# Turning normed attention inputs by 32x32 blocks and a trip through memory instead of on the matrix engine

## The chip, the cores and the metric

The kernel runs on one core of a Trainium2 chip. The metric is the device time of one execution in microseconds (us). Before the change it is 941.15 us, the median of three runs (940.75 to 942.05).

A core has a matrix engine (TensorE, PE in the profile, PEld for its weight loads), three engines for elementwise work (VectorE or DVE, ScalarE or ACT, GpSimd or POOL), a queue engine (SyncE or SP) that issues transfers here, and sixteen DMA engines that carry them. Each engine works through its own instructions in order; semaphores tie them together.

## The reference

For each of 16 batches (256 tokens, 256 features, 16 heads of 16) three attentions follow one another, and a feed-forward layer ends it. All is float32.

```python
x0  = rmsnorm(x + softmax(rms(x)Wq (rms(y)Wk)' * scale) rms(y)Wv Wo)   # layer 0: cross attention
h   = layernorm(x0);  q, k, v = h@sa_w...;  rope(q), rope(k)
x1  = x0 + softmax(causal(q k' * scale)) v @ sa_wo                     # layer 1: causal, on itself
h   = layernorm(x1);  q = h@ca_wq;  k, v = y@ca_w...;  rope(q), rope(k)
x2  = x1 + softmax(q k' * scale) v @ ca_wo                             # layer 2: cross attention
out = x2 + gelu(layernorm(x2)@fc1) @ fc2
```

## The kernel before, in words

There are 48 attentions (3 layers x 16 batches), worked off in a list `ORDER` of layer numbers written by hand, in one loop `for i in range(N_ATT)`. After it come eight feed-forward groups of two batches. The emission order is the order of each engine: the schedule is manual.

In loop `i` TensorE does attention `i` in blocks: four score blocks for layers 0 and 2, three for the causal layer 1 (L472 scores, then L511 values of the block before). A non-causal loop takes 15.2 to 16.2 us, a causal one 13.3. Between the blocks it does the dense work of neighbouring attentions:

- block 0: the last values of `i-1`; on VectorE, the statistics (L236, L237; on POOL L218, L219) of `i+2`, the copy of the values of `i-1` out of PSUM (L528), the normalization of `i+2` (L243), and the division of `i-2` (L562). Then the queries of `i+1` (`by_feature`, L274), with their rotation on VectorE (L386 to L408).
- block 1: the keys of `i+1` (L274, rotation to L431); the inverse of the softmax sums of `i-1` (L548).
- next to last block: the values' weights of `i+1` (`by_token`, L287, L452).
- last block: the output projection of `i-2` (L287, added by L568 or L571), then the **turn** of `i+2`.

In a loop whose attention `i-3` was of layer 0 (`finishing`) that one's last scaling (L576) comes in block 0, and the normalization of `i+2` in block 1.

The turn matters here. The dense matmuls want the input with features on partitions (`hT`), but layernorm (`ln_apply`) leaves tokens on partitions (`xn`). For layers 1 and 2, `turned` makes four 128x128 transposes on TensorE into a PSUM bank (L254) and a ScalarE copy into `hT` (L259), a tile `[P, KC, S]` in two buffers. Layer 0 needs none: its input comes already turned from the host. So 32 attentions have a turn. The queries of layers 1 and 2 and the keys and values of layer 1 read `hT`; keys and values of layer 2 read `yT`.

The head outputs and the softmax sums go through memory, by SP: stores of the values (L529), reads of the sums (L536) and of the head outputs (L541), a store of the inverted sums (L550) and its spread reads (L556). Inputs of later batches and weights are issued on SP in `load_next` (L903), right after the reads of L541 and again in block 1.

The buffers: `A`, where values accumulate, has one PSUM bank, freed by L528. Score tiles have two. Dense results have three banks. Tile `a`, in which rotations start, has two buffers.

Of the kernel before, what the change touches and what calls it, by code (L numbers as in the profile page):

```python
# [32 lines left out]
PT_LIVE = 6  # L33

# [8 lines left out]
SWAP = [(i // HD) * HD + (i + HD // 2) % HD for i in range(32)]  # L43

@with_exitstack
def xattn_kernel(
# [202 lines left out]
    def turned(src, name, pool, tag, bufs):  # L249

        ps = dense_ps()
        for c in range(NC):
            for k in range(KC):
                nc.tensor.transpose(  # L254
                    ps[:, k * S + c * P : k * S + (c + 1) * P],
                    src[:, c, k * P : (k + 1) * P], ident,
                )
        t = pool.tile([P, KC, S], F32, tag=tag, name=name, bufs=bufs)
        nc.scalar.copy(t.rearrange("p k s -> p (k s)"), ps)  # L259
        return t  # L260

# [6 lines left out]
    def by_feature(src, w, at, ts=range(KC)):  # L268

        ps = dense_ps()  # L270
        for t in ts:
            for k in range(KC):
                for j in range(0, P, 32):
                    nc.tensor.matmul(  # L274
                        ps[j : j + 32, t * S : (t + 1) * S],
                        lhsT=w[:, k, at + t * P + j : at + t * P + j + 32], rhs=src[:, k, :],
                        start=(k == 0), stop=(k == KC - 1), skip_group_check=True,
                    )
        return ps.rearrange("p (t s) -> p t s", s=S)

    def by_token(src, w, at):

        ps = dense_ps()
        for c in range(NC):
            for k in range(KC):
                for j in range(0, P, 32):
                    nc.tensor.matmul(  # L287
                        ps[j : j + 32, c * D : (c + 1) * D],
                        lhsT=src[:, k, c * P + j : c * P + j + 32], rhs=w[:, k, at : at + D],
                        start=(k == 0), stop=(k == KC - 1), skip_group_check=True,  # L290
                    )
        return ps.rearrange("p (c d) -> p c d", d=D)


    class Att:
        def __init__(self, i):
            self.i = i
            self.layer = ORDER[i]
            self.b = ORDER[:i].count(self.layer)
            self.causal = self.layer == 1  # L300
            self.w = (w0_sb, sa_sb, ca_sb)[self.layer]
            self.w_o = (w0o_sb, sao_sb, cao_sb)[self.layer]
            self.x = rows_of(self.b)
            self.va = vas[i % 2]


            if self.causal:
                self.blocks = [[(0, 0)], [(0, 1), (1, 1)], [(1, 0)]]
                self.parts = [[(0, 0)], [(0, 1)], [(1, 1), (1, 0)]]
            else:  # L310
                self.blocks = [[(t, kc)] for t in range(KC) for kc in range(NC)]
                self.parts = self.blocks
            self.pts = {}
# [56 lines left out]
        def turn(self):  # L370
            if self.layer == 0:
                self.hT = xTs.pop(self.b)
            else:
                self.hT = turned(self.xn, "hT", work, "hT", 2)
            self.kvT = self.hT if self.layer == 1 else yTs[self.b]
# [207 lines left out]
    def att(i):  # L583
        if 0 <= i < N_ATT:
            return atts.setdefault(i, Att(i))
        return None
# [43 lines left out]
    class Mlp:  # L630
# [15 lines left out]
        def turn(self, copy=nc.scalar.copy):  # L646
            self.hT = self.pool.tile([P, KC, 2, S], F32, tag="qm", name="hT3")
            for i, xn in enumerate(self.xns):
                ps = dense_ps()
                for c in range(NC):  # L650
                    for k in range(KC):
                        nc.tensor.transpose(  # L652
                            ps[:, k * S + c * P : k * S + (c + 1) * P],
                            xn[:, c, k * P : (k + 1) * P], ident,
                        )
                copy(self.hT[:, :, i, :], ps.rearrange("p (k s) -> p k s", s=S))

        def mix(self, tag="av"):
# [5 lines left out]
            else:  # L664
                pairs = [self.pool.tile([P, 2, S], F32, tag=tag, name="ts") for _ in range(2)]
# [196 lines left out]
    with tc.manual_schedule():  # L862
# [42 lines left out]

        for i in range(N_ATT):
            a, last = att(i), att(i - 1)
            ahead = att(i + 3)
            if i > 1 and ahead is not None and ahead.layer == 0:
# [5 lines left out]
            follows = (  # L915
                finishing and i + 2 < N_ATT
                and att(i + 2).layer == 1 and att(i + 2).b == att(i - 3).b
            )
            for n in range(len(a.blocks)):
                if n == 0 and a.causal and not finishing:  # L920
                    do(i + 2, "stats")
# [6 lines left out]
                if n == 0:  # L928
# [4 lines left out]
                    if not follows and not late and (finishing or not a.causal):  # L933
                        do(i + 2, "stats")
                    do(i - 1, "end")
                    load_next(i)
                    if late:
                        do(i + 2, "stats")
                    do(i - 3, "finish")
                    if follows:  # L940
                        do(i + 2, "stats")
                    if not finishing:
                        do(i + 2, "norm")
# [9 lines left out]
                elif n == 1:  # L953
# [11 lines left out]
                    if finishing:  # L965
                        do(i + 2, "norm")
# [5 lines left out]
                if n == final - 1:  # L972
                    do(i + 1, "v")
                    if i == N_ATT - 2:
                        mlps[1].stats()
                    if i == N_ATT - 1:
                        mlps[0].up(2)
                        mlps[0].mix("hT")
                if n == final:
# [4 lines left out]
                    do(i + 2, "turn")  # L984
# [16 lines left out]
                if i == 2 and n == 2:  # L1001
                    att_cols = fold_back(att_hop)
                    row_v = ctile([P, D], "row_v")
# [505 lines left out]
```

## Time and profile before

| | |
|---|---|
| median of three runs | 941.15 us |
| the profiled execution | 940.73 us |
| its span (first to last instruction) | 939.0 us |
| TensorE busy | 929.7 us |
| VectorE / ScalarE / POOL busy | 662.7 / 547.1 / 311.4 us |
| turns on TensorE (L254) | 128 transposes, 272 to 330 ns each, overlapping |
| copies of turned inputs (L259) | 32, 586 ns each |
| normalization (L243) | 96 of 593 ns |
| statistics (L236, L237) | 96 of 405 ns, 96 of 182 ns |
| matmuls that read `hT` (L274) | 1,536 of 379 ns each, overlapping |
| transfers | 83.2 MB in 98,989 packets |

The busy time of an engine is the union of its instructions. Matmuls overlap: four that write different groups of 32 partitions run at once, so what one costs is read from the distance between starts, not from its duration. The profile follows a chain back from the last instruction: at each step to what released it, or to the instruction before it on its engine. A loop's length is read from the timeline of TensorE, as the distance between the first L472 of one attention and of the next.

### The profile page before, as it was taken

The page shows a single profiled execution, that of the slowest core. Times are in us where ns is not written, and L with a number is a line of the kernel's source. Part 1 is how long each engine was busy: PE and PEld are TensorE (multiplying, and loading weights), DVE is VectorE, ACT ScalarE, POOL GpSimd, SP SyncE. Part 2 cuts the span into 40 slices and gives each one's busy share as a digit, 9 for nine tenths or more (in the row PEclk, how much of TensorE's full clock was granted, in tenths as well). Part 3 has the DMA queues.
Part 4 walks back from the last instruction along what each step waited for, and adds up shares of the span by engine and source line. Part 5 has one row for each costly group of instructions (what it writes and reads, how often), then busy time and mean ns, then how long its engine had stood idle before and what let it go on. Part 6 is the DMA issues. An engine that isn't in the chain of part 4 may idle for free.

```text
span 939.0 us, 29252 instructions
## 1 busy us (share of the span) xinstructions
PE 929.7 (99%) x12358; PEld 548.6 (58%) x12358; DVE 662.7 (71%) x1440; ACT 547.1 (58%) x772; POOL 311.4 (33%) x503
## 2 busy tenths in 40 slices
PE   8999999999999999999999999999999999999997
PEld 3444555445454455455454545455444799999997
DVE  4458776867777787868866768888787576667663
ACT  3666655766666665656656666666666634444440
POOL 4213454125444364253542324445133021222200
PEclk9999999999999999999999999999999999999999
DMA  9434353333333233321443322222212100000001
GB/s 292 155 102 129 120 161 114 118 110 95 110 99 95 82 104 100 106 91 58 136 127 97 110 83 63 79 72 82 82 60 82 38 23 23 13 12 24 24 24 48
DMA packets 98989, 83.20 MB, mean 89 GB/s; under 512 B 21658, under 2 KB 98594, under 8 KB 98850
## 3 DMA queue, kind: packets, MB, share of 16 engines
q1 hardware_dynamic: 98162, 80.70, 27.4%
q8 instruction: 99, 1.62, 0.7%
q10 hardware_dynamic: 688, 0.54, 0.2%
q14 instruction: 40, 0.33, 0.1%
HBM read 51.05 MB, written 30.17 MB: 86 GB/s over the span
## 4 chain that ended last, share of the span: by engine, by line
PE 98%; DMA 1%; DVE 0%; SPq 0%; POOL 0%; issue 0%; ACT 0%; DVEq 0%
PE S L472 20%; PE A L511 19%; PE d L287 17%; PE d L274 17%; PE upX L676 6%; PE A L774 5%; PE downZ L774 3%; PE upZ L676 3%; PE d L254 2%; PE d L774 2%; PE d L676 1%; PE d L652 1%; PE downX L774 1%; DMA y<-in_y 1%; PE d L172 0%; SPq L107 0%
## 5 line engine op out<-in xcount | busy, mean ns | idle before, releaser
L483 ACT ACTIVATE pt<-S 128x1024 f32<-128x1024 f32 x224 | 217.3, 1022 | 120.4 <-PE S L472 120.2
L472 PE MATMUL S<-qm,kT 32*128 32x512 f32 (+1 forms) x1536 | 202.4, 600 | 0.7 <-DVE qm L422 0.4
L511 PE MATMUL A<-pt,va 128*32 128x256 f32 (+1 forms) x3072 | 188.7, 367 | 0.0
L511 PEld LDWEIGHTS A<-pt,va 128*32 128x32 f32 x3072 | 80.0, 109 | 153.4 <-issue 107.1
L483 ACT ACTIVATE pt<-S,sy 128x1024 f32<-128x1024 f32 x128 | 135.8, 1111 | 47.1 <-PE S L472 46.2
L490 POOL TENSOR_SCALAR_AFFINE_SELECT pt<-pt 128x512 f32<-128x512 f32 x128 | 90.3, 721 | 60.1 <-ACT pt L483 59.6
L472 PEld LDWEIGHTS S<-qm,kT 32*128 32x128 f32 x1536 | 62.3, 183 | 66.6 <-issue 40.8
L218 POOL TENSOR_SCALAR r_ln<-bmv 128x2 f32<-128x2 f32 x48 | 13.9, 290 | 217.0 <-DVE bmv L237 215.8
L263 POOL TENSOR_TENSOR cur<-cur,bias 128x512 f32<-128x512 f32 x48 | 66.1, 1382 | 56.5 <-DVE xn L243 56.5
L382 ACT ACTIVATE a<-d,qk_bias 128x256 f32<-128x256 f32 x128 | 53.7, 471 | 51.3 <-PE d L274 39.5
L274 PE MATMUL d<-hT,sa 128*32 128x256 f32 x1024 | 61.1, 379 | 0.0
L571 DVE TENSOR_TENSOR cur<-d,cur 128x512 f32<-128x512 f32 x32 | 22.0, 687 | 50.7 <-PE d L287 50.7
L528 DVE COPY av<-A 128x512 f32<-128x512 f32 x47 | 32.3, 687 | 30.4 <-PE A L511 29.9
L243 DVE TENSOR_SCALAR xn<-cur,bmv,r_ln 128x256 f32<-128x256 f32 x96 | 52.2, 593 | 1.4 <-POOL r_ln L219 0.8
L390 DVE TENSOR_TENSOR u<-u,turn 128x512 f32<-128x512 f32 x64 | 49.7, 777 | 0.0
L390 DVE TENSOR_TENSOR a<-a,turn 128x512 f32<-128x512 f32 x64 | 47.3, 739 | 2.2
L714 ACT ACTIVATE g<-g,fb 128x256 f32<-128x256 f32 x96 | 41.0, 500 | 11.1 <-DVE g L703 11.1
L386 DVE STREAM_SHUFFLE u<-a 128x512 f32<-128x512 f32 x64 | 47.5, 742 | 0.0
L274 PEld LDWEIGHTS d<-hT,sa 128*32 128x32 f32 x1024 | 33.3, 110 | 22.0
L218 POOL TENSOR_SCALAR r_o<-ms_o 128x2 f32<-128x2 f32 x16 | 3.9, 243 | 125.6 <-DVE sq L226 116.0
L562 DVE TENSOR_TENSOR oT<-oT,inv 128x512 f32<-128x512 f32 x48 | 39.6, 824 | 5.8 <-DMA inv<-inv_hop 5.8
L769 DVE TENSOR_TENSOR g<-g,g 128x512 f32<-128x512 f32 x64 | 40.9, 682 | 0.0
(149 smaller groups left out, 1566.4 us busy)
## 6 DMA issues: line engine op xcount, KB each, us to landing
hop<-av SPq DMA_DIRECT2D x96, 256.0 KB
oT<-hop SPq DMA_DIRECT2D x96, 128.0 KB
inv<-inv_hop SPq DMA_DIRECT2D x96, 128.0 KB
xT<-in_xt SPq DMA_DIRECT2D x16, 256.0 KB
cur<-in_x SPq DMA_DIRECT2D x16, 256.0 KB
yT<-in_yt SPq DMA_DIRECT2D x16, 256.0 KB
y<-in_y SPq DMA_DIRECT2D x16, 256.0 KB
out<-res SPq DMA_DIRECT2D x15, 256.0 KB
```

The lines of the kernel that those rows point to most:

```text
L243: nc.vector.tensor_scalar(xn[:, c, :], src[:, c, :], mv[:, c, 0:1], r[:, c : c + 1], ALU.subtract, ALU.mult,)
L263: nc.gpsimd.tensor_tensor(t, t, bias_sb[:, row : row + D].unsqueeze(1).to_broadcast([P, NC, D]), ALU.add)
L274: nc.tensor.matmul(ps[j : j + 32, t * S : (t + 1) * S], lhsT=w[:, k, at + t * P + j : at + t * P + j + 32], rhs=src[:, k, :], start=(k == ...
L287: nc.tensor.matmul(ps[j : j + 32, c * D : (c + 1) * D], lhsT=src[:, k, c * P + j : c * P + j + 32], rhs=w[:, k, at : at + D], start=(k == ...
L382: nc.scalar.activation(a[:, t], ps[:, t], AF.Identity, bias=bias[:, t : t + 1])
L390: nc.vector.tensor_tensor(t, t, table.unsqueeze(1).to_broadcast([P, KC, S]), ALU.mult)
L472: nc.tensor.matmul(ps[:, j, 2 * m * u : 2 * m * (u + 1)] .rearrange("p (i s) -> p i s", i=2), lhsT=self.kT[r, t, kc * P : (kc + 1) * P], r ...
L483: nc.scalar.activation(pt[:, :, :w], ps[:, :, :w], AF.Exp, scale=scale)
L490: nc.gpsimd.affine_select(out=diag, in_=diag, compare_op=ALU.is_ge, fill=0.0, base=0, pattern=[[0, 2], [0, 2], [1, P]], channel_multiplier=-1,
L511: nc.tensor.matmul(self.av[32 * r : 32 * r + 32, i, q0:S], lhsT=self.va[:, kc, 8 * t + 2 * r + i, :], rhs=pts[r // 2][:, r % 2, i * m : (i ...
L676: nc.tensor.matmul(banks[c // 2][:, (c % 2) * S : (c % 2 + 1) * S], lhsT=a[:, c * P : (c + 1) * P], rhs=b, start=(first and c % 2 == 0), s ...
L774: nc.tensor.matmul(ps[:, c, :], lhsT=a[f // 2][:, f % 2, c * P : (c + 1) * P], rhs=b[:, f, :], start=(first and c == 0 and f == 0), stop=True,
```

## The change

`turned_ahead` pairs attentions that need a turn with earlier loops, three to seven ahead, that are not causal and lie late enough after the attention that makes their input. It finds 23 pairs, here as loop: attention.

```
4:7 6:9 8:11 10:13 11:16 12:15 15:19 17:21 18:23 20:26 22:25 24:28
25:29 27:30 29:33 30:35 32:37 34:39 36:41 37:40 39:42 41:44 43:46
```

For these, the statistics come in block 0 of the sending loop: ahead of the copy L528, or, where the input was made three attentions before (`fresh`), after it and ahead of the division. In the next to last block, after the values' weights of `i+1`, `pieces_out` normalizes, makes two 32x32-block transposes on VectorE (128x256 each) into a tile `a`, and stores 256 KB to memory. In block 0 of the next loop, after the reads L541 and ahead of `load_next`, `pieces_in` issues four reads of 64 KB, each of which gathers the blocks of 32 features. Statistics, normalization and turn in the loop two ahead fall away for these 23. Attentions 5, 12, 18, 22, 31, 38, 43, 45 and 47 keep the turn on TensorE.

`hT` has a new order `[P, 4, KC, NC, 32]`, for both kinds of turn: a partition's tokens lie in runs of 32. Matmuls that take it as moving operand (`all_tokens`) read eight such runs; those that take it as weights (`some_tokens`) read one. It has three buffers. To make room, `row_v` uses a part of `fc2_sb` before that is loaded.

```diff
+HT_LIVE = 3
+def attended(j):
+    b = ORDER[:j].count(ORDER[j])
+    return b, [i for i in range(N_ATT) if ORDER[i] == ORDER[j] - 1][b] if ORDER[j] else None
+def turned_ahead():
+    slots = {}
+    def place(j, tried):
+        for m in range(j - 3, max(attended(j)[1] + 2, j - 8), -1):
+            if ORDER[m] != 1 and m not in tried:
+                tried.add(m)
+                if m not in slots or place(slots[m], tried):
+                    slots[m] = j
+                    return True
+        return False
+    for j in range(N_ATT):
+        if ORDER[j] > 0:
+            place(j, set())
+    return slots
...
+    def turned(src):
+        ps = turn_ps(src)
+        t = turn_tile()
+        nc.scalar.copy(
+            t.rearrange("p q k c i -> p (k c) q i"),
+            ps.rearrange("p (k q i) -> p k q i", q=4, i=32),
+        )
         return t
+    def all_tokens(src, k, like=None):
+        if len(src.shape) == 3:
+            return src[:, k], like
+        if like is not None:
+            like = like.rearrange("p (c q i) -> p c q i", c=NC, i=32)
+        return src[:, :, k].rearrange("p q c i -> p c q i"), like
+    def some_tokens(src, k, c, j):
+        if len(src.shape) == 3:
+            return src[:, k, c * P + j : c * P + j + 32]
+        return src[:, j // 32, k, c, :]
...
+        def pieces_out(self):
+            self.norm()
+            t = work.tile([P, 4, KC, NC, 32], F32, tag="a", name="turn")
+            for k in range(KC):
+                nc.vector.transpose(
+                    t[:, :, k].rearrange("p g c i -> p c g i"),
+                    self.xn[:, :, k * P : (k + 1) * P].rearrange("p c (g j) -> p c g j", j=32),
+                )
+            self.turn_hop = dram.tile([P, 4, KC * NC * 32], F32, tag="turn", name="turn_hop")
+            nc.sync.dma_start(
+                out=self.turn_hop, in_=t.rearrange("p g k c i -> p g (k c i)")
+            )
+        def pieces_in(self):
+            self.hT = turn_tile()
+            hop = self.turn_hop.rearrange("(q j) g f -> g j q f", j=32)
+            for g in range(4):
+                nc.sync.dma_start(
+                    out=self.hT[32 * g : 32 * g + 32].rearrange("p q k c i -> p q (k c i)"),
+                    in_=hop[g],
+                )
             self.kvT = self.hT if self.layer == 1 else yTs[self.b]
...
+            sent, due_turn = turns.get(i), i + 2 if i + 2 not in turns.values() else None
+            fresh = sent is not None and att(sent).below == i - 3
...
-                        do(i + 2, "stats")
+                        do(due_turn, "stats")
+                    if sent is not None and not fresh:
+                        do(sent, "stats")
                     do(i - 1, "end")
+                    do(turns.get(i - 1), "pieces_in")
                     load_next(i)
                     if late:
-                        do(i + 2, "stats")
+                        do(due_turn, "stats")
                     do(i - 3, "finish")
                     if follows:
-                        do(i + 2, "stats")
+                        do(due_turn, "stats")
+                    if fresh:
+                        do(sent, "stats")
                     if not finishing:
-                        do(i + 2, "norm")
+                        do(due_turn, "norm")
...
                 if n == final - 1:
                     do(i + 1, "v")
+                    do(sent, "pieces_out")
...
-                    do(i + 2, "turn")
+                    do(due_turn, "turn")
```

## The prediction, on record before the changed kernel ran

> **What bounds the kernel now.** I read the page's busy shares first, then the chain of work that ended last, then TensorE's timeline around one turn.
>
> ```profile
> PE 929.7 (99%) x12358; PEld 548.6 (58%) x12358; DVE 662.7 (71%) x1440; ACT 547.1 (58%) x772; POOL 311.4 (33%) x503
> PEclk9999999999999999999999999999999999999999
> PE 98%; DMA 1%; DVE 0%; SPq 0%; POOL 0%; issue 0%; ACT 0%; DVEq 0%
> PE S L472 20%; PE A L511 19%; PE d L287 17%; PE d L274 17%; PE upX L676 6%; PE A L774 5%; PE downZ L774 3%; PE upZ L676 3%; PE d L254 2%; PE d L774 2%; PE d L676 1%; PE d L652 1%; PE downX L774 1%; DMA y<-in_y 1%; PE d L172 0%; SPq L107 0%
> ```
>
> TensorE (PE) is busy 99% of the span at a granted clock that never dips, and 98% of the chain is its own instructions. The view of who waited for whom lists under 5 us of waiting on it in all. So every instruction taken off TensorE shortens the kernel by its place in the stream, until something else is late. The turns (L254) hold 2% of the chain. The timeline of all engines shows one, at the end of attention 26's loop:
>
> ```profile
> 410.21 1.14 PE L472 MATMUL S<-qm,kT 32*128 32x512 f32 x8
> 411.74 1.91 PE L287 MATMUL d<-w0o,oT 128*32 128x256 f32 x32
> 413.58 0.66 PE L254 MATMUL d<-ident,xn 128*128 128x128 f32 x4
> 414.17 1.14 PE L472 MATMUL S<-qm,kT 32*128 32x512 f32 x8
> ```
>
> Columns: start, length, engine, line. The next loop's scores start 0.59 us after the turn's four transposes start. In all 32 turns this distance is 0.585 to 0.588 us. The lengths of whole loops, from first score to first score, say the same: 15.78 us with a turn and 15.19 without, 16.22 and 15.63 after a causal attention. Causal loops all have a turn and take 13.29.
>
> **What the change removes.** 23 turns: 92 transposes on TensorE, 23 x 0.586 = 13.5 us, all on the path. ScalarE loses 23 copies of 0.586 us (L259), 13.5 us off the path. What is late next at that place? The scores need both score buffers, which the exponentials free: in loop 26 they end at 413.39 (411.45 + 1.94) and the scores would now start at 413.58, so 0.19 us is left. The 15.63 us loops of layer 0, where the exponentials are longest (1.11 us against 1.02) and no turn follows, show no wait there. I count the full 13.5.
>
> **What it adds on VectorE (DVE).** Per turn two 32x32 transposes of 128x256. The trace has the operation only at 128x32, and a shuffle through the same kind of 32-row exchange at 128x512:
>
> ```profile
> L348 DVE STREAM_TRANSPOSE pad<-pad x14: 152/154/200, 18.6 to 527.1; 128x32 f32<-128x32 f32 x14
> L386 DVE STREAM_SHUFFLE u<-a x64: 714/745/765, 79.8 to 707.0; 128x512 f32<-128x512 f32 x64
> ```
>
> A straight line through 154 and 745 ns gives 0.43 us at 256 columns, so 0.86 us a turn. Bounds: 2 x 0.154 from below, 2 x 0.745 from above; I take 0.86, between them on the line, which makes 19.8 us in all (662.7 to 682). The statistics (four instructions, 1.22 us) and the normalization (2 x 0.593) of the attention sent ahead are not new; they move from its own loop, two ahead, to an earlier non-causal one. A sending loop thus gains 1.22 + 1.19 + 0.86 = 3.27 us, and the loop two before the turned attention loses 2.4. The page of the skill that speaks against this is "VectorE: DVE Perf Modes" of the Trainium skill, section "Rules for kernel authors": for 128x128 it prefers TensorE, and its section "The three transpose paths" gives 390 ns there and 311 ns on VectorE, in bf16. By these, an estimate from the page, a turn would be worth 4 x 0.39 = 1.56 us of TensorE and all of them 35.9 us. The trace shows 0.586 us a turn, and that decides.
>
> Does VectorE have 3.27 us? The table of stretches gives its work per loop (row: stretch, its length, then busy times):
>
> ```profile
> 73.81:89.00 15.19, 15.19 (x229) 7.08 (x228) 13.82 (x38) 11.22 (x14) 6.30 (x10) 1.00 0.31 96
> 89.00:102.29 13.29, 13.29 (x220) 7.10 (x216) 8.71 (x22) 6.89 (x8) 7.87 (x14) 1.00 0.47 142
> 327.24:340.53 13.29, 13.29 (x217) 7.10 (x216) 11.49 (x22) 8.57 (x12) 8.35 (x12) 1.00 0.27 81
> 459.92:475.11 15.19, 15.19 (x229) 7.08 (x228) 12.99 (x32) 10.50 (x14) 6.18 (x10) 1.00 0.37 118
> 475.11:488.40 13.29, 13.29 (x220) 7.10 (x216) 7.62 (x15) 6.88 (x8) 6.43 (x12) 1.00 0.37 117
> ```
>
> These are loops 4, 5, 21, 30 and 31. Loops 4 and 30 both send; they have 1.4 and 2.2 us free, so about 1.9 and 1.1 us spill over. The causal loops after them have 4.6 and 5.7 us free and lose another 2.4 us of work. Three results of VectorE can stop TensorE, and I read the spare time of each from the timeline. **First**, the copy that frees the only value bank (L528, then L511): done 1.45 us early in loops 5, 7, 9 and 1.2 to 1.98 us early in the others. The spill of loop 4 reaches it, but the statistics of attention 7, which stood ahead of that copy in loop 5, are gone (1.22 us), so 1.9 - 1.2 = 0.7 us of 1.45 is used. **Second**, the rotated keys (L431), the last thing before the next scores. They are done early by 1.10 us (loop 4), 1.40 (6), 1.73 (15), 0.15 (22), 2.01 (29), 1.40 (30), and 2.0 to 4.3 in the other senders. The moved statistics stand ahead of them and take 1.22. Loop 4 then misses by 0.1; loop 22 starts about 1.8 us sooner, because loop 21 (11.49 of 13.29 us busy) loses 2.4 us of work and 0.59 us of length, and so keeps some 0.7; loop 30's spill from 29 falls into its own 1.03 us gap before the value copy. **Third**, the values' stationary side (L452), 4 to 8 us early. The two small POOL instructions of the statistics (L218, L219, 1.08 us) move with them, to loops where POOL has 6 us and more free. The normalization and the transposes stand behind all three, ahead of the projection's add (L571), where VectorE waits 0.6 to 3.1 us for TensorE. So nearly all is hidden. One operation stretched by neighbours (L406 takes 1.65 us in loop 4, 0.69 elsewhere) can uncover some 0.7 us in one of the tight loops: I charge 0.7 us.
>
> **What it adds on the transfers.** 115 issues on SP: per turn one of 256 KB out, four of 64 KB in. An issue takes about 0.65 us (L541, two in 1.30), so 3.2 us a turn. The one out waits for the transposes; behind it is the next loop's value store, whose copy stands behind the transposes on VectorE anyway. The four in stand behind the two reads of the head outputs and ahead of the sums' inverse, at 408.24 and 409.35 in loop 26:
>
> ```profile
> 406.94 1.30 SPq L541 DMA_DIRECT2D oT<-hop  x2
> 409.35 0.34 SPq L550 DMA_DIRECT2D inv_hop<-sums  x1
> 410.93 1.22 SPq L556 DMA_DIRECT2D inv<-inv_hop  x2
> 418.28 1.75 DVE L562 TENSOR_TENSOR oT<-oT,inv 128x512 f32<-128x512 f32 x1
> ```
>
> 1.1 us of the 2.6 fit in the gap; the inverse is 1.5 us later, and its user (L562) comes 6.1 us after the last issue, against about 2.3 us to land (as the value store of 404 to 406). The tightest is loop 33, with 3.0 us and two loads already in the gap: there the inverse lands some 1.8 us after VectorE wants it, which the 2.96 us of loop 34's keys less 1.22 just cover. The waits for a buffer of hT never bite: with three, the one reused was read at least half a loop before. Per turn 1024 packets of 512 bytes at 42 ns (4,117 us of engine time over 98,162 packets) add 62 us over 16 engines, 6.6% of the span to 27.4%. I cost the transfers at nothing. Covered by: the time until the queries are made. Where an attention is sent exactly three ahead and the loop between is causal (nine cases), the four issues would end at 100.0 in loop 5 (97.4 + 2.6), land at 102.3, and be read at 104.1: 1.8 us spare there, up to 3.2 elsewhere.
>
> **What it does to TensorE's reads.** hT now lies as 32-column runs. The moving operand of 1,536 instructions (L274 with hT) crosses seven breaks; no row has runs that short. The nearest: in causal loops 16 score matmuls of 256 columns in two runs of 128 take 1.08 us (404.68 to 405.76) for the same columns as 8 unbroken ones in 1.07. One break costs nothing. As the other end, each run could cost as much as a matmul of its own: 16 value matmuls take 0.46 us at 128 columns and 0.89 at 256, so 2 x 28.8 - 55.6 = 2 ns a piece, 14 ns an instruction, 1,536 x 14 = 21.5 us. I take nothing, by the nearer row. SBUF: State Buffer of the Trainium skill (in "Door 1: The DMA port swizzle") counts 16-byte lines, of which a run here fills eight; no run here shows it.
>
> **Sum.** The profiled execution took 940.73 us, 1.73 more than its span of 939.0, and 0.42 less than the median 941.15. 940.73 - 13.5 + 0.7 = 927.9; on the median's scale **928.4 us**.
>
> **Rivals.**
> 1. *VectorE late.* If the spare time of the following loop cannot be used, what exceeds a sender's own idle time stops TensorE: 1.9 us (loop 4), 0.6 (6), 0.3 (15), 1.0 (20), 0.4 (22), 0.8 (29), 2.1 (30, whose 1.03 us gap lies ahead of the statistics), 1.2 (43), sum 8.3. 940.73 - 13.5 + 8.3 + 0.42 = 936.0. For it: 13.82 of 15.19 us busy in loop 4. Against: the relief in the causal loop after it. Chance 0.17.
> 2. *Pieces land late.* With issues at L550's slowest (1.09 us, 4 x 0.45 more) and landings at the longest wait for a value store (4.3 us, 2.0 more) the nine close cases are 3.8 us later against some 2.7 spare: 9 x 1.1 = 9.9, so 937.6. For: SP already waits 105.8 us for value stores. Against: both extremes at once. Chance 0.10.
> 3. *Broken reads are slow*, the one on the other side: TensorE pays 21.5 us on L274, so 940.73 - 13.5 + 0.7 + 21.5 + 0.42 = 949.9. It decides from 8.8 ns an instruction (13.5 us over 1,536), 15% of the 57.5 that each has. Against: the 128-column row. Chance 0.08.
> 4. *It does not do what it says*: the removed 0.586 us was cover for the exponentials and score buffers, and a wait on ScalarE takes its place: 941. Against: 15.63 us loops. Chance 0.05.
>
> The forecast keeps 0.60. The range reaches from the full gain and a microsecond of today's small waits (926.5) through rivals 1 and 2 to 938; it leaves out rivals 3 and 4 and part of 2, under 0.2. A measurement of this kernel can tell 0.2% (1.9 us) from no change; by the same cases faster is 0.86, no change 0.05, slower 0.09.
>
> **What will show it.** L254 falls from 128 to 36 transposes; causal loops shrink from 13.29 to 12.70 us; L274 with hT keeps 379 ns and 1.73 us per 32; VectorE's transposes take 0.43 us; TensorE's list of waits stays under 6 us. Wrong if L274 grows, if waits for L431, L528 or hT appear on TensorE, or if the two transposes take over 1.2 us.

## The result and the profile after

The changed kernel takes 938.25 us (median of 21 runs, 935.70 to 945.62) where the kernel before takes 941.15 (21 runs, 940.59 to 942.95). The ratio is 0.9977, 95% interval 0.9964 to 0.9990: faster by 2.2 us (the medians lie 2.9 apart), not by the 12.7 us of the forecast (928.4), and 0.25 us outside the range's upper end, 938. The profiled execution took 935.70 us with a span of 933.8; that of before took 940.73 and 939.0.

The page of the changed kernel, busy shares, clock and chain of work that ended last:

```profile
PE 920.2 (99%) x12266; PEld 540.2 (58%) x12266; DVE 679.2 (73%) x1486; ACT 533.2 (57%) x749; POOL 314.0 (34%) x503
PEclk9999999999999999999999999999999999999999
PE 78%; DVE 11%; DMA 5%; issue 2%; SPq 2%; POOL 2%; ACT 1%; DVEq 0%
```

TensorE (PE) has 92 matmuls fewer, VectorE (DVE) 679.2 us where the prediction had 682, and the clock is as before. The share "99%" of TensorE has not moved and says nothing. The third line does: of the chain that sets the end only 78% is TensorE's own work, where it was 98%. VectorE, transfers and POOL now hold 18% of it.

The two prices that the prediction had bounded, from the view of the transposes' line (ns, shortest, median and longest) and from the costliest groups (busy us, mean ns):

```profile
L436 DVE STREAM_TRANSPOSE turn<-xn x46: 401/424/448, 89.9 to 663.7; 128x256 f32<-128x256 f32 x46
```

```profile
L329 PE MATMUL d<-hT,sa 128*32 128x256 f32 x1024 | 61.1, 379 | 0.0
```

The 32x32 transposes take 0.424 us (predicted 0.43). A matmul that reads `hT` in eight runs of 32 columns takes the 379 ns that it took in one run, and the 32 of a block start within 1.53 us in both kernels: the rival of slow broken reads is gone.

**Where the gain went.** TensorE's list of waits shows almost nothing:

```profile
PE S L551 <- DVE kT L510: 3.6, 8, 0.9
...
PE A L590 <- POOL pt L569: 0.7, 3, 0.2
```

These sums are too small, since a matmul whose weights come late is busy in pieces, and its wait stands under its weight load (PEld). The lengths of the 48 loops, from first score to first score, miss nothing. I took each loop's length in the two profiles, and 0.586 us off before's where a turn is gone; what the loop takes beyond that is its excess. The table of stretches of the changed kernel (stretch, length, busy times of PE, PEld, VectorE, ScalarE and POOL) has three kinds, here loops 5, 13 and 28:

```profile
88.75:102.52 13.77, 13.38 (x209) 6.79 (x209) 8.94 (x20) 6.61 (x8) 6.55 (x12) 1.00 0.52 149
210.01:222.71 12.70, 12.70 (x213) 6.68 (x209) 7.27 (x14) 6.61 (x8) 6.18 (x12) 1.00 0.47 124
428.91:442.04 13.13, 12.76 (x213) 6.70 (x209) 10.10 (x16) 7.98 (x11) 6.78 (x10) 1.00 0.35 111
```

Loop 13 is what was forecast for a causal loop, 12.70 us, and five others are like it. Loop 5 is *longer* than the 13.29 of before. Loop 28 is 0.43 over. In the profiled execution:

| place | loops | excess, us |
|---|---|---|
| masks of a causal loop late on POOL | 5, 7, 23 (+1.07 each), 9 (+0.86) | 4.1 |
| keys late in a loop that lost its statistics | 21, 28, 38, 40, 42 (+0.43 each) | 2.15 |
| keys late in or after a sending loop | 6 (+1.01), 22 (+0.56), 12, 43, 30, 4 (+0.20 to +0.42) | 2.7 |
| all others | 11 (-0.14) | -0.1 |

So 23 x 0.586 = 13.5 us less 8.8 us, and 0.4 us at the start (10.07 us to the first score instead of 10.50; 10.88 in run e1, so this moves by itself), give the 5.2 us between the two spans but for 0.1. The other runs of the changed kernel are on the median 2.5 us slower than that one, and lie 10 us apart where before's lie 2.4 apart. A second profile (run e1, 940.52 us) has the same excess to 0.01 us in loops 5, 7 and 23 and in the five of the second row, and more than the first in loops 8 (+2.45), 9 (+1.69 in all), 12 (+1.51 in all) and 16 (+0.88).

**Late masks.** The timeline of loop 5 of the changed kernel, which starts at 88.75 us:

```profile
89.12 0.73 DVE L271 TENSOR_SCALAR xn<-cur,bmv,r_ln 128x256 f32<-128x256 f32 x2
89.88 0.77 DVE L436 STREAM_TRANSPOSE turn<-xn 128x256 f32<-128x256 f32 x2
90.58 0.65 DVE L647 TENSOR_TENSOR s<-d,cur 128x512 f32<-128x512 f32 x1
92.26 0.22 POOL L246 TENSOR_SCALAR r_o<-ms_o 128x2 f32<-128x2 f32 x1 [8.30 <-DVE sq L254]
...
93.23 1.42 POOL L569 TENSOR_SCALAR_AFFINE_SELECT pt<-pt 128x512 f32<-128x512 f32 x2
...
93.93 1.61 PE L590 MATMUL A<-pt,va 128*32 128x256 f32 x14 [0.24 <-POOL pt L569]
```

and the same place before, in a loop that starts at 88.97:

```profile
89.11 0.69 DVE L568 TENSOR_TENSOR s<-d,cur 128x512 f32<-128x512 f32 x1 [0.64 <-PE d L287]
...
91.81 1.48 POOL L490 TENSOR_SCALAR_AFFINE_SELECT pt<-pt 128x512 f32<-128x512 f32 x2
...
93.85 1.07 PE L511 MATMUL A<-pt,va 128*32 128x256 f32 x16
```

The normalization and the transposes that loop 4 sends run into loop 5 and stand ahead of the add of attention 2's projection (0.14 us into the loop before, 1.83 now). Behind the add come its mean squares, behind these the root `r_o` on POOL, and behind the root, in POOL's own order, the causal masks of the loop: 2.84 us into the loop before, 4.48 now. The values that read the masked scores took 1.07 us for 16 matmuls; now 14 take 1.61 and the last two come after them. They end 5.95 us into the loop before and 7.02 now: the 1.07 us of excess. POOL is 34% busy. Its share says nothing of this; its order does.

**Late keys.** The timeline of loop 28 of the changed kernel (428.91 to 442.04):

```profile
433.77 0.01 DVE L465 LOAD_MASK_SELECT u<-a  x1 [1.34 <-ACT a L461]
...
440.88 1.01 DVE L510 TENSOR_TENSOR kT<-a,u 128x512 f32<-128x512 f32 x1
...
442.04 1.14 PE L551 MATMUL S<-qm,kT 32*128 32x512 f32 x8 [0.37 <-DVE kT L510]
```

The rotation of the queries starts 4.86 us into the loop, after VectorE has waited 1.34 us for ScalarE's copy of the queries out of PSUM, and the keys are done 12.98 us into it. Before, with the loop's start at 430.39:

```profile
435.20 0.01 DVE L386 LOAD_MASK_SELECT u<-a  x1 [0.67 <-ACT a L382]
442.31 1.01 DVE L431 TENSOR_TENSOR kT<-a,u 128x512 f32<-128x512 f32 x1
```

The two places were 4.81 and 12.93, in a loop of 13.29. The statistics and the normalization that left this loop had filled gaps ahead of the rotation; without them the gaps are larger (1.34 us instead of 0.67) and nothing is earlier. The chain scores, queries, copy, rotation, keys takes 13 us with that work and without it. The keys were only 0.36 us early before, so the loop can give 0.16 of its 0.586 us.

### The profile page after: what moved, and what is told of

Same layout as the page of the kernel before. It is cut to its first block, busy times and chain, and to the rows that moved or that the text cites. A ratio compares the mean times of both kernels' runs of the same rounds, so it can differ in the third digit from the quotient of the medians.

```text
span 933.8 us, 29304 instructions
## 1 busy us (share of the span) xinstructions
PE 920.2 (99%) x12266; PEld 540.2 (58%) x12266; DVE 679.2 (73%) x1486; ACT 533.2 (57%) x749; POOL 314.0 (34%) x503
## 3 DMA queue, kind: packets, MB, share of 16 engines
q1 hardware_dynamic: 114722, 92.77, 31.8%
q8 instruction: 98, 1.61, 0.7%
## 4 chain that ended last, share of the span: by engine, by line
PE 78%; DVE 11%; DMA 5%; issue 2%; SPq 2%; POOL 2%; ACT 1%; DVEq 0%
PE S L551 15%; PE A L590 14%; PE d L341 13%; PE d L329 13%; PE upX L752 6%; PE A L850 5%; PE downZ L850 3%; PE upZ L752 3%; DVE u L469 2%; PE d L850 2%; DVE a L469 2%; PE d L752 2%; DVE u L465 1%; PE d L286 1%; DMA hop<-av 1%
## 5 line engine op out<-in xcount | busy, mean ns | idle before, releaser
L590 PE MATMUL A<-pt,va 128*32 128x256 f32 (+1 forms) x3072 | 191.2, 367 | 1.3 <-POOL pt L569 0.7
L317 POOL TENSOR_TENSOR cur<-cur,bias 128x512 f32<-128x512 f32 x48 | 68.7, 1438 | 56.5 <-DVE xn L271 56.5
L246 POOL TENSOR_SCALAR r_ln<-bmv 128x2 f32<-128x2 f32 x48 | 15.3, 318 | 118.0 <-DVE bmv L265 116.5
L469 DVE TENSOR_TENSOR u<-u,turn 128x512 f32<-128x512 f32 x64 | 52.2, 816 | 0.0
L469 DVE TENSOR_TENSOR a<-a,turn 128x512 f32<-128x512 f32 x64 | 49.8, 777 | 2.2
L271 DVE TENSOR_SCALAR xn<-cur,bmv,r_ln 128x256 f32<-128x256 f32 x96 | 41.5, 481 | 0.8 <-POOL r_ln L247 0.8
```

Of the source, the lines that this page charges most:

```text
L317: nc.gpsimd.tensor_tensor(t, t, bias_sb[:, row : row + D].unsqueeze(1).to_broadcast([P, NC, D]), ALU.add)
L469: nc.vector.tensor_tensor(t, t, table.unsqueeze(1).to_broadcast([P, KC, S]), ALU.mult)
L590: nc.tensor.matmul(self.av[32 * r : 32 * r + 32, i, q0:S], lhsT=self.va[:, kc, 8 * t + 2 * r + i, :], rhs=pts[r // 2][:, r % 2, i * m : (i ...
```

## The experiments

Twelve runs. Diffs are against the changed kernel, but for the last. Each median stands beside that of the kernel before, measured with it.

**e1: the changed kernel once more.** No edit.

> The changed kernel once more, unaltered, for a second profile. The first profile (935.7 us) was its fastest execution; the 21 runs spread from 935.7 to 945.6 with a median of 938.25, those of the kernel before only from 940.6 to 943.0. Theory A, fixed waits (a late square root ahead of the causal masks on POOL, 4.1 us; key chains in five causal loops, 2.2 us; late keys in six other loops, 2.7 us): these three come again within 0.3 us each, and what this execution has beyond 935.7 lies in waits that end with a transfer. Rival, no fixed places: the lost microseconds lie in other loops than in the first profile.

Measured: 939.72 us (937.86 to 945.43) beside 941.97, ratio 0.9983 [0.9967, 0.9999]. The fixed places of the table above come back; the rest moves from run to run. One cause of the moving part is a load that lands late: in loop 8 VectorE waits 2.06 us for `x` (shown under e10).

**e2: the root later.** Only the root moves, so that POOL's masks don't stand behind it.

```diff
 def project(self):
-    self.ro = inv_sqrt(mean_squares(self.s0, "o"), EPS_RMS, "o")
+    self.ms = mean_squares(self.s0, "o")
 def finish(self):
+    self.ro = inv_sqrt(self.ms, EPS_RMS, "o")
```

> The inverse root of the projection's mean squares (two small POOL instructions) is emitted where it is used, in the next loop's block 0, behind that loop's first causal masks. Nothing else changes. Theory A: loops 5, 7, 9 and 23 lose the wait of the values on the masks and fall from 13.8 to 12.7 or 12.8 us, so 3 to 4 us faster than the changed kernel, about 934.5 us median. Rival, VectorE late in general: the loops stay at 13.5 us or more, because the copy of the values comes late as well, and the time moves by less than 1 us.

Measured: 948.62 us (946.51 to 951.09) beside 941.97, ratio 1.0070 [1.0055, 1.0085]. Loops 7 and 23 lose their excess and loop 9 keeps 0.12, so the masks did wait for the root there. But loop 5 rises to +2.86, loops 4, 8 and 30 to +3.3 or more, and the time got worse, which I had not expected. From the list of who waited for whom in this run:

```profile
DVE cur L656 <- POOL r_o L247: 22.2, 13, 3.1
```

VectorE now stops for the root (22.2 us in 13 waits; 2.1 us in 4 in the changed kernel), and the keys behind it in VectorE's order are late: 12.0 us of TensorE's waits instead of 3.6. The wait was moved, not removed.

**e3: the new way left out.** Statistics and normalization are sent ahead as in the changed kernel; transposes, store and reads are left out, and the 23 attentions read another tile.

```diff
-    do(sent, "pieces_out")
+    do(sent, "norm")
 def pieces_in(self):
-    self.hT = turn_tile()
...
+    self.hT = yTs[self.b]
```

> The 23 sent turns are left out: no 32x32 transposes, no transfers out and in; these attentions read the y tile of their batch instead of the turned input. Statistics and normalization stay where the change puts them. Theory A: five causal loops (21, 28, 38, 40, 42) still take 13.1 us and not 12.7, because the rotation of the next keys and not the statistics fills them; the other losses shrink with 0.86 us of VectorE less: 930 us median, and a spread as small as before the change (2 us). Rival 1, the transfers cost everything: 927.7. Rival 2, the moved statistics and normalization cost most: 935 or more.

Measured: 931.95 us (930.26 to 934.32) beside 941.97, ratio 0.9894 [0.9880, 0.9909]: 10.0 of the 13.5 us. The five loops of the second place still take 13.07 us (+0.37), with nothing but the statistics and the normalization moved. Loops 5, 7 and 23 are down to +0.28. So with this order of statistics and normalization the ceiling was some 10 us, not 13.5.

**e4: one read instead of four.** The store spreads the blocks, and one transfer of 256 KB fetches them.

```diff
-nc.sync.dma_start(out=self.turn_hop, in_=t.rearrange("p g k c i -> p g (k c i)"))
+hop = self.turn_hop.rearrange("(g j) q f -> q j g f", j=32)
+for q in range(4):
+    nc.sync.dma_start(
+        out=hop[q], in_=t[32 * q : 32 * q + 32].rearrange("p g k c i -> p g (k c i)"),
+    )
...
-for g in range(4):
-    nc.sync.dma_start(
-        out=self.hT[32 * g : 32 * g + 32].rearrange("p q k c i -> p q (k c i)"),
-        in_=hop[g],
-    )
+nc.sync.dma_start(
+    out=self.hT.rearrange("p q k c i -> p (q k c i)"),
+    in_=self.turn_hop.rearrange("p q f -> p (q f)"),
+)
```

> Memory layout of the hop changed: four stores of 32 partitions in the sending loop and one read of 2 KB per partition in the next, instead of one store and four reads; 640 packets instead of 1,024 a turn, and 1.8 us of SP less ahead of the inverse of the sums. Theory, transfers in the way of the inverse: the waits of the division for the inverse (13.0 us in all in the first profile) fall back towards the 5.8 of before, loop 6 loses its 1.0 us, and the spread shrinks: 1 to 3 us faster than the changed kernel. Rival, order of SP does not matter: within 0.5 us of the changed kernel; or slower by 1 us, if four stores ahead of the next value store delay that one.

Measured: 940.81 us (935.28 to 946.24) beside 941.97, ratio 0.9995 [0.9976, 1.0013]. No gain, and the runs lie 11 us apart. VectorE's waits for the inverted sums did fall, to 6.3 us (13.0 in the changed kernel, 5.8 before), as the theory asked, and the time didn't follow. The run doesn't clear the four reads by itself, since four stores now stand where one stood.

**e5: loads first.** `load_next` goes ahead of the four reads.

```diff
-    do(turns.get(i - 1), "pieces_in")
     load_next(i)
+    do(turns.get(i - 1), "pieces_in")
```

> In block 0 the loads of the next batch (load_next) are issued ahead of the four reads of the turned pieces, and not behind them. Nothing else changes. Theory B, the part that varies from run to run is transfers: in the second profile loop 8 lost 2.45 us and loop 9 1.69, because VectorE waited 2.06 us for a load of x that SP issued behind the four reads. With the loads 1.8 us sooner that wait goes in most runs: median 936.5 to 938.5, spread under 6 us. Rival, the loads are late because the value store lands late behind the 256 KB store of the turn: the wait on x stays, and the median stays within 1 us of the changed kernel (938 to 940).

Measured: 941.25 us (936.13 to 945.31) beside 941.82, ratio 0.9991 [0.9976, 1.0007]. No gain: in the profiled execution loops 6, 8, 9, 12 and 34 have an excess of 1.5 to 2.3 us each. In loop 8 VectorE no longer waits for `x`, but waits 3.03 us for the inverted sums (23.0 us in all loops): the wait has moved, as in e2.

**e6: pieces after the projection.** Normalization, transposes and store go behind the projection's add.

```diff
 do(i + 1, "v")
-do(sent, "pieces_out")
...
 do(i - 2, "project")
+do(sent, "pieces_out")
```

> Normalization, block transposes and the store of the sent attention are emitted one block later, behind the projection of i-2, so that the projection's mean squares and their root on POOL are not held up. Theory A: loops 5, 7, 9 and 23, now 13.77 us because the causal masks queue on POOL behind the late root, fall to 13.0 or less: 3 us faster than the changed kernel where no transfer is late (best run near 933). Rival: the copy of the values (L607) takes the delay instead, and the same loops wait on it for 1 us each: within 1 us of the changed kernel.

Measured: 940.08 us (938.28 to 945.22) beside 941.82, ratio 0.9988 [0.9972, 1.0004]. Loops 5, 7 and 23 have no excess and loop 9 has 0.09: what made the masks late was the order of add and transposes on VectorE. The median doesn't show it, since two other things grew. The transposes now stand later, ahead of the copy that frees the value bank, and TensorE waits for that:

```profile
PE A L590 <- DVE av L607: 3.4, 3, 1.7
```

(0.95 us each in loops 18 and 25), and loops 8 and 12 have +3.04 and +1.37. In loop 8 VectorE waits 3.96 us for the load of `x`.

**e7: eighteen turns.** The five turns whose loops gave only 0.16 us stay on TensorE.

```diff
-    return slots
+    return {m: j for m, j in slots.items() if (ORDER[j - 2], ORDER[j - 1]) != (1, 2)}
```

> Five of the 23 pairs are dropped: attentions 23, 30, 40, 42 and 44, whose TensorE turn stood in a causal loop that is filled by the rotation of the next keys (loops 21, 28, 38, 40, 42). They turn on TensorE as before the change. Theory A: each of these turns earned 0.15 us and not 0.59, so dropping all five costs 0.8 us or less in these loops, and what the sending loops 18, 27, 37, 39 and 41 and the transfers get back is worth about as much: the median within 1 us of the changed kernel. Rival, every turn earns its 0.586 us: 2.9 us slower.

Measured: 941.86 us (939.29 to 946.07) beside 941.82, ratio 1.0000 [0.9987, 1.0012]. Loops 28, 38, 40 and 42 are back at 13.29 to 13.32 us, where the turn's removal had made them 13.13: each of these turns is worth 0.16 to 0.19 us. The median can't be read for it: the profiled execution lost 1.3 to 2.7 us in each of loops 8, 12, 21 and 34 to the part that moves from run to run.

**e8: e5 and e6 together.**

> The two moves together: loads ahead of the reads of the pieces, and normalization, transposes and store behind the projection. Theories A and B: both gains add up, median 933 to 936 and a smaller spread than 10 us. Rival: the store of the turn now stands right ahead of the next value store, which lands later still, and the median is no better than the better one of the two moves alone.

Measured: 942.14 us (938.56 to 947.75) beside 941.82, ratio 1.0003 [0.9986, 1.0020]. With the store later and the reads later, TensorE waits for the pieces themselves (4.8 us in 3 waits; 2.0 in e5), the second rival's mechanism, which the changed kernel doesn't show.

**e9: no transfers.** Transposes stay, the store and the reads are left out.

```diff
-    self.turn_hop = dram.tile([P, 4, KC * NC * 32], F32, tag="turn", name="turn_hop")
-    nc.sync.dma_start(out=self.turn_hop, in_=t.rearrange("p g k c i -> p g (k c i)"))
+    self.turn_t = t
...
 def pieces_in(self):
-    self.hT = turn_tile()
...
+    self.hT = yTs[self.b]
```

> As the run with the turn left out (931.95 us), but the normalization and the two 32x32 transposes are done in the sending loop; only the store to memory and the four reads are left out, and the attentions read the y tile of their batch. It splits the 7.8 us between that run and the changed kernel. Theory, both count: the causal masks in loops 5, 7, 9 and 23 wait as in the changed kernel (1.07 us each against 0.28), so about 935 us, and the rest, some 4.5 us and the spread, is the transfers. Rival 1, VectorE alone: 939. Rival 2, transfers alone: 932 to 933.

Measured: 932.60 us (932.29 to 933.90) beside 940.77, ratio 0.9909 [0.9895, 0.9924]. Beside e3 the transposes cost some 1.4 us (0.0015 of 941, with intervals that overlap). Loops 5 and 23 are back at +1.07, but loop 7 has no excess and loop 9 has 0.33: there the full wait shows only with transposes and transfers together. Loops 8, 12 and 34, which lose 1 to 4 us in some executions with transfers, lose nothing here; loop 16 loses 0.89 all the same. The four runs lie 1.6 us apart, but the five of e3, which has no such transfers either, 4.1, so how much of the spread is the transfers' is not shown.

**e10: the store of the turn behind the value store.** The one edit: the 256 KB store is issued after the second half of the value store instead of between its halves.

```diff
 def pieces_out(self):
...
+    self.turn_t = t
+
+def pieces_store(self):
+    t = self.turn_t
     self.turn_hop = dram.tile([P, 4, KC * NC * 32], F32, tag="turn", name="turn_hop")
     nc.sync.dma_start(out=self.turn_hop, in_=t.rearrange("p g k c i -> p g (k c i)"))
...
-def end(self, copy=nc.vector.tensor_copy):
+def end(self, copy=nc.vector.tensor_copy, beside=lambda: None):
     self.take(1, copy)
+    beside()
...
-do(i - 1, "end")
+if last is not None:
+    last.end(beside=lambda: do(turns.get(i - 1), "pieces_store"))
```

> The store of the sent turn is issued behind the second value store of the next loop (between it and the reads of the sums) instead of ahead of it. The same bytes move; the reads of the pieces keep their place. Theory B, the store of the turn delays the value store, whose landing starts the chain sums, inverse, division, queries, keys: the time from the value store's issue to the read of the sums falls back towards the 1.9 us median of before the change (2.4 to 2.5 now, up to 4.4 in loops 5, 7, 13 and 23), and the median falls by 2 to 4 us, to 936 or 937. Rival, the reads and the loads are what crowds the engines: within 1 us of the changed kernel; if the reads now wait for the store to land, 1 to 2 us slower.

Measured: 934.09 us (933.18 to 934.80) beside 940.77, ratio 0.9926 [0.9913, 0.9939], five runs 1.6 us apart. This is the largest term of all: 0.9977 to 0.9926 is 4.8 us of 941, from the place of one store in one queue, and the two intervals don't meet. SP's timeline in loop 7 shows it. Before (start, length of the issues, line):

```profile
118.65 3.05 SPq L529 DMA_DIRECT2D hop<-av  x2
123.64 0.55 SPq L536 DMA_DIRECT2D sums<-hop  x1
```

In e1, the changed kernel:

```profile
122.14 0.41 SPq L608 DMA_DIRECT2D hop<-av  x1
122.60 0.47 SPq L441 DMA_DIRECT2D turn_hop<-turn  x1
123.11 0.50 SPq L608 DMA_DIRECT2D hop<-av  x1
128.00 0.55 SPq L615 DMA_DIRECT2D sums<-hop  x1
```

and in e10:

```profile
121.14 1.72 SPq L612 DMA_DIRECT2D hop<-av  x2
122.89 0.54 SPq L445 DMA_DIRECT2D turn_hop<-turn  x1
125.95 0.55 SPq L618 DMA_DIRECT2D sums<-hop  x1
```

The read of the sums waits until the value store has landed. From the end of the second half's issue to that read it takes 1.9 us before, 4.4 in e1, 3.1 in e10 (3.4 in e9, so not all of the rise is the store's). Over all 48 loops the median of this distance is 1.91 us before, 2.39 in the changed kernel, 2.48 in e1, 1.93 in e10. In the 23 loops behind a sending one it is 1.88 before, 2.35 in the changed kernel, 2.38 in e1, 1.89 in e10, and 1.89 and 1.91 in e9 and e3, which have no such store. The other 25 loops lie at 2.4 to 2.6 us with the store (changed kernel, e1) and without (e9, e3), at 2.2 before and in e10, so only the half microsecond behind the senders is surely the store's. Behind that read stand on SP the head outputs, the four reads of pieces, and the loads of the next inputs, which come later too. SP's total wait for the value stores is no measure of this, here of the changed kernel and of e10:

```profile
SPq L615 <- DMA hop<-av: 120.0, 49, 4.7
```

```profile
SPq L618 <- DMA hop<-av: 97.0, 48, 4.7
```

It was 105.8 us before, but 115.3 in e9 and 118.0 in e3, where no such store stands, and in e10 the store's own issues take up a part of it. Nor do VectorE's waits for the inverted sums rank the runs: 5.8 us before, 13.0 in the changed kernel and 7.4 in e10, but 13.4 in e11 at 933.29 us and 6.3 in e4 at 940.81. What shows the loss is, in single executions, a load of `x` that comes too late, as in loop 8 of e1:

```profile
135.54 0.43 DVE L254 SCALAR_TENSOR_TENSOR sq<-cur 128x256 f32<-128x256 f32 x1 [2.06 <-DMA cur<-in_x]
```

Loop 8's keys are then 2.31 us late. Its load was issued 13.0 us into loop 7 in e1, 11.3 in e10 and 7.6 before. This holds across the profiles: where VectorE waits 1.5 to 4.0 us for `x` in loop 8 (e1, e2, e4, e6, e7, e8, e11), the loop has an excess of 2.0 to 4.0 us; where it waits 0.5 us or less (the first profile of the changed kernel, e3, e9, e10, e12), it has none. Only e5 loses there by the inverted sums instead.

"DMA: Bandwidth & Descriptors" of the Trainium skill, in "Queues, rings and completion order", says that a transfer's semaphore is raised only after every earlier write of the same DMA engine. By that rule a store that stands ahead must land before the second half of the value store counts as landed. The runs agree in sign (half a microsecond more with the store ahead, nothing with it behind), but none of them separates this rule from the bandwidth that the two stores share.

**e11: e10, and behind the projection where e6 helped.** In loops whose attention `i-2` is of layer 0, normalization and transposes go behind the projection; elsewhere they stay.

```diff
-    do(sent, "pieces_out")
+    if i < 2 or att(i - 2).layer:
+        do(sent, "pieces_out")
...
     do(i - 2, "project")
+    if i >= 2 and not att(i - 2).layer:
+        do(sent, "pieces_out")
```

> The store behind the value store, and in loops whose projection is of layer 0 the normalization and transposes behind that projection (elsewhere ahead of it, since loops 18 and 25 lost 0.95 us each with it). Theories A and B: loops 5, 7, 9 and 23 lose their wait on the masks (4 us), and the chain from the value store is shorter: 933 to 935 us. Rival: the transposes now stand between the projection and the copy of the values, so loops 6 and 8 wait for that copy and the gain is under 1.5 us.

Measured: 933.29 us (930.93 to 935.26) beside 940.77, ratio 0.9914 [0.9900, 0.9927]. Loops 5, 7 and 23 have no excess. Against e10 it is 0.0012 better, with intervals that overlap; the profiled execution gave 2.35 and 1.63 us back in loops 8 and 9. In loop 8 the load of `x` came 1.48 us late. This is the lowest median of the runs that do the whole work; e3 and e9, which leave parts of the new way out, are lower.

**e12: the transfers alone.** The kernel before, with 23 stores of 256 KB and 92 reads of 64 KB that nobody uses, at the places where the changed kernel has its own (and with `row_v` in `fc2_sb`, as there).

```diff
+def spare_out(i):
+    hops[i] = dram.tile([P, 4, P], F32, tag="turn", name="turn_hop")
+    nc.sync.dma_start(out=hops[i], in_=turn_sb.rearrange("p (g f) -> p g f", g=4))
+
+def spare_in(i):
+    hop = hops[i].rearrange("(q j) g f -> g j q f", j=32)
+    for g in range(4):
+        nc.sync.dma_start(out=spare[32 * g : 32 * g + 32], in_=hop[g])
...
 do(i - 1, "end")
+if i - 1 in turns:
+    spare_in(i - 1)
 load_next(i)
...
 do(i + 1, "v")
+if i in turns:
+    spare_out(i)
```

> The kernel before the change with the 23 stores of 256 KB and 92 reads of 64 KB added at the places of the change; they store the rotation table and read into a spare tile that nobody uses. All 32 turns stay on TensorE, statistics and normalization stay in their loops; nothing waits for these transfers but the queue. Theory B: 3 to 5 us slower than before, at a larger spread, by late sums and inverses. Rival, the transfers hurt only together with the late VectorE: under 1 us slower.

Measured: 941.99 us (940.21 to 944.82) beside 940.77, ratio 1.0015 [1.0005, 1.0025]: 1.4 us, between the theory's 3 to 5 and the rival's under 1. The median from value store to read of the sums is 1.92 us, as before (1.89 behind a sending loop). So neither the 115 issues nor the bytes cost much by themselves. Here the store doesn't wait for anything and is out 2.9 us (median) ahead of the second half of the value store; in the changed kernel it goes out when the transposes are done, 1.8 us ahead, and in loop 7 of e1 0.04.

## Why the prediction was wrong

The steps, in the prediction's order:

- *"I count the full 13.5"*: right for what leaves TensorE. Causal loops without another limit shrink to 12.70 us as forecast; but in five loops another limit stood 0.36 us away (fourth point). No wait for the exponentials took the place of the turns, so the fourth rival is out.
- *"A straight line ... gives 0.43 us at 256 columns"*: right, 0.424.
- *"I take nothing, by the nearer row"* for the broken reads: right, 379 ns.
- *"loop 21 ... loses 2.4 us of work and 0.59 us of length, and so keeps some 0.7"*: wrong. VectorE's lost work lay in gaps ahead of a chain that starts on TensorE. Loops 21, 28, 38, 40 and 42 gave 0.16 us each: 2.15 us missing. The prediction looked for late keys in the senders, and took the loops that lose work to be relieved. e3 has these 2 us with neither transposes nor transfers, e7 gives them back.
- *"Three results of VectorE can stop TensorE"*: there is a fourth, by way of POOL. The prediction wrote that the transposes stand ahead of the projection's add, and that the two small POOL instructions move to loops with room. It didn't follow the add's other user, the root, into POOL's order ahead of the masks: 4.1 us. e6 removes it, e2 shows that the root is the link. By e9 the transposes do this alone in loops 5 and 23, and reach the full wait in loops 7 and 9 only with the transfers.
- *"I charge 0.7 us"* for one tight loop: too small; late keys in and after the sending loops cost 2.7 us, of which loop 6 has 1.0. In e9, with all of VectorE's added work and no transfers, loop 6 has none, in e10 0.4 and in e3 0.5, so more than half of it is not that work's.
- *"behind it is the next loop's value store, whose copy stands behind the transposes on VectorE anyway"* and *"I cost the transfers at nothing"*: wrong, and the largest. The prediction asked when the store is issued, and not when the one behind it has landed. e10 puts it at 4.8 us; e9 and e10 together, 0.9909 to 0.9926, leave some 1.6 us for the transfers otherwise. The amount of transfer was not mis-sized downwards: a turn has 720 packets and not 1,024, the packets' share of the 16 DMA engines' time rose from 27.4% to 31.8% and not by 6.6 points, and the four reads are issued in 1.83 us (loop 7) and not 2.6.

By ratio, from no transposes and no transfers to the changed kernel, 941 us each:

| | ratio | us beside the 13.5 |
|---|---|---|
| turns gone, statistics and normalization moved (e3) | 0.9894 | -3.5 |
| and transposes on VectorE (e9) | 0.9909 | -1.4 |
| and transfers, store behind the value store (e10) | 0.9926 | -1.6 |
| and the store between its halves (the change) | 0.9977 | -4.8 |

The rows add up to 11.3 of 13.5, and 2.2 us are left, as the ratio has it; they must, being differences of one another. Each ratio is known to some 1.3 us either way and the differences less well, so the two in the middle say only that these terms are small. The second rival (937.6) came nearest in size, by luck: it named transfers, but pieces that land late are not in the changed kernel's waits. The first (VectorE late, 936.0) was half right in mechanism: what exceeded a sender's idle time did reach the next loop, but stopped TensorE by way of POOL. Two smaller slips bear on nothing here: no row gives the 1.73 us that it names for 32 matmuls that read `hT` (they start within 1.53 us and are done after 1.91 in both kernels), and the listed chances give 0.87 for faster and not 0.86.

**What stays open.** Which transfer is late in a given execution, and so why loops 8, 9, 12, 16 and 34 lose 1 to 4 us in some and nothing in others: e10's profile has 0.76 in loop 9 and nothing in the others, e11's has 2.35 and 1.63 in loops 8 and 9, with the store at the same place. By what path the late landing becomes the whole 4.8 us is seen for loop 8 alone. Whether the store delays the value store by the order of completions or by bandwidth was not tried apart.

## What to carry to other kernels

Price a transfer put into a queue by the landing of the next one behind it too, above all where a chain of memory trips starts there: here one store's place is worth 4.8 us. For a VectorE result that becomes late, follow every user into its own engine's order, also on an engine that is a third busy. Work that leaves an engine helps only where it stood on the chain: compare the time from the loop's start to the last result, not the busy sums, and look for the next limit (here 0.36 us away) before a removed piece is counted in full.

## What the runs showed of the hardware

- A fp32 transpose in 32x32 blocks takes VectorE 0.424 us for 128x256, in line with 0.154 for 128x32 and 0.745 for a shuffle of 128x512.
- A moving operand in runs of 32 fp32 columns costs TensorE nothing here: 1,536 matmuls at 379 ns, 32 of them started within 1.53 us, in one run or in eight.
- 23 stores of 256 KB and 92 reads of 64 KB, on top of 83 MB, cost 1.4 us where the store is out 2.9 us ahead of the one that starts a chain (e12), and with the store closer ahead of that one (1.8 us, median) the kernel is 4.8 us slower than with it behind (e10).
- Idle time on TensorE hides from its own list of waits when it is the weights that are late: for the masks 0.7 us stood under PE and 15.8 under PEld (1.7 before), much of that hidden: the four loops lost 4.1, and e6 still has 11.7 where they lose at most 0.09.
